# A two-layer scan kernel: the second layer's instructions in an order written out by hand, side work cut into small pieces, ten of sixteen states fed through TensorE

## The chip, the cores and the metric

The kernel runs on one core of a Trainium2 chip. A core has four engines that compute, each with its own instruction queue that is worked through strictly in order: TensorE (PE: matrix multiplies and transposes, with its weight loads shown apart as PEld), VectorE (DVE), ScalarE (ACT) and GpSimd (POOL). SyncE (SP) issues the DMAs. The metric is the device time of one execution in microseconds (us). Everything is float32.

## The reference, cut to what matters

There are two layers over an input of 2 batches x 2048 positions x 256 features. Layer 0 (a gated scan and a routed feed-forward) is not touched by the change. Layer 1 is a pair of selective scans, forward and backward in time, each over 512 channels with 16 states, followed by a norm, and two feed-forwards:

```python
xz = x @ Win;  xi, z = split(xz);  xi = silu(conv4(xi))       # depthwise, causal
dt = softplus((xi @ Wx)[:16] @ Wdt + bdt);  Bm, Cm = (xi @ Wx)[16:32], [32:48]
def step(h, u_t, dt_t, B_t, C_t):              # h: 512 channels x 16 states
    h = exp(dt_t * A) * h + (dt_t * u_t) * B_t
    return h, einsum('ds,s->d', h, C_t)
y = (scan(step) + u * D) * silu(z) @ Wout      # then layernorm, for both directions
out = layernorm(ff(yf + yb) + yf + yb) + x + gelu_ff(x)
```

## The kernel before

Layer 1 (function `layer1`, L495) handles time in chunks of T = 512 positions. Its **16 steps** are, for each of 2 batches, 4 chunks forward and 4 chunks backward (L630 to L635). A step has K = 64 **iterations**, one per pair of a state n (16) and a block e of 128 channels (4). An iteration is one 128x512 recurrence on VectorE (`scan`, L825, the instruction at L836).

Around each recurrence:

- `decay` (L797) makes exp(dt * A) on ScalarE (L806).
- `source` (L808) makes the input term dt * u * B. There are **two kinds of iteration**. In kind D, GpSimd multiplies `dtu` by a broadcast row of B (L823); the decay lies in PSUM, and the recurrence writes over it. In kind P ("turned B"), ScalarE first scales the transposed `dtuT` by a column of B (`scaled`, L788, at L792, four pieces per state, each serving four channel blocks), and TensorE transposes the result back into PSUM (L816, four 128x128 transposes); the recurrence writes to SBUF.
- After the recurrence its last column is copied to `hn`, for the next chunk (kind P: GpSimd, L844; kind D: ScalarE, L847), and the result is multiplied by a broadcast row of C (kind P: GpSimd, L845; kind D: VectorE, L848).
- `collect` (L850), some iterations later, adds the product to the output by four accumulating transposes on TensorE (L870).

Iterations come in eight blocks m of 8 (two states x four channel blocks). `kinds` (L755) says which kind each state has: DD, then six times PD (alternating), then PP. PSUM has eight banks: four for the output accumulators (`yacc`), two for side work (`pp`), and **two (`ab`) for the iterations**: the bank of iteration g is filled again for g+2 only when the recurrence of g (in kind D, also its C product) is over.

**Side work** goes between the iterations: `finish_parts` (L1063) of the step before (transposes, the output projection, norms and, where that step was a backward one, two halves of both feed-forwards, `ff_parts`, L925), `prepare_parts` (L1034) of the step after (gate and input projections, convolution, Silu, projections to dt, B, C, Softplus), a `prologue` in steps 4 to 7, and `late_parts` (L1056). Each part carries a weight, and the loop at L1094 to L1144 emits parts so that the weights are spread over iterations 5 to 55; `late_parts` is emitted at iteration 56. Steps 5 to 8 and 13 to 15 thus hold the feed-forwards of a backward chunk; I call them **ff steps**, and the others **plain steps**.

What is emitted is not yet the order on the engines: the tile framework's **planner** reorders the instructions of each engine by emission order, readiness and an estimate of costs, and allots the buffers. Decays are emitted 4 iterations ahead (kind P) or 1 ahead (kind D), sources 1 ahead, `collect` 4 behind.

Of the kernel before, what the change touches and what calls it, by code (L numbers as in the profile page):

```python
# [18 lines left out]
P = 128  # L19
# [475 lines left out]
def layer1(tc, c, a, x1d, wupd, wdnd, bupd, out):  # L495
    nc = c.nc
    with ExitStack() as ctx:
# [78 lines left out]
        zero = wp.tile([P, P], F32, name="zero")  # L576
        nc.gpsimd.memset(zero, 0.0)
        ident4 = c.ident.unsqueeze(1).broadcast_to([P, 4, P])
# [68 lines left out]
        def gate(ck, zs, tb):  # L647

            ps = c.pp()
            for k in range(2):  # L650
                nc.tensor.matmul(
                    ps, ck.xnT[:, k, tb * P : (tb + 1) * P], ck.w["winz"][:, k, :],
                    start=(k == 0), stop=(k == 1),
                )
            nc.scalar.copy(zs[:, tb, :], ps)

        def conv(i, e):
# [5 lines left out]
            ps = c.pp()  # L663
            for k in range(2):
                nc.tensor.matmul(
                    ps, w["winx"][:, k, e * P : (e + 1) * P], ck.xnT[:, k, :],
                    start=(k == 0), stop=(k == 1),
                )
# [11 lines left out]
            for k in range(3):  # L680
                o = 3 - k if bw else k
                nc.vector.scalar_tensor_tensor(  # L682
                    ck.u[:, e] if k == 2 else ps, xi[:, o : o + T], pk[:, e, k : k + 1], ps,
                    ALU.mult, ALU.add,
                )
# [5 lines left out]

        def project(i):
            ck = steps[i]
            ps = c.pp()
            for e in range(4):
                nc.tensor.matmul(  # L696
                    ps, ck.w["wx"][:, e, :], ck.u[:, e, :], start=(e == 0), stop=(e == 3)
                )
            ck.par = ap.tile([P, T], F32, tag="par", name="par", bufs=1)
            nc.scalar.copy(ck.par, ps)  # L700
            ck.bcd = c.dram.tile([80, T], F32, tag="bcd", name="bcd", bufs=3)
            nc.sync.dma_start(ck.bcd[32:80, :], ck.par[32:80, :])
# [52 lines left out]
        kinds = ["DD"] + ["PD"] * 6 + ["PP"]  # L755
# [9 lines left out]
        lo, hi = 0, 8  # L765
        for n in range(NS):
            ks = [k for k in range(K) if plan[k][1] == n and plan[k][3] == "P"]
            if ks:
                for q in range(TB):
                    fills[lo + q * (hi - lo) // TB].append((n, q))  # L770
                lo, hi = ks[0], ks[-1] + 1
# [25 lines left out]
        def decay(g):  # L797
# [4 lines left out]
            if kind == "P":  # L802
                r["a"] = sp.tile([P, T], F32, tag="a", name="a", bufs=5)
            else:
                r["a"] = r["ps"] = c.ab()
# [19 lines left out]
        def scan(g):  # L825
# [15 lines left out]
            gt = r["g"] = sp.tile([P, T], F32, tag="g", name="g", bufs=6)  # L841
            hn = ck.hn[:, e, n : n + 1]
            if kind == "P":
                nc.gpsimd.tensor_copy(hn, h[:, last : last + 1])  # L844
                nc.gpsimd.tensor_mul(gt, h, ck.cb[n])  # L845
            else:
                nc.scalar.copy(hn, h[:, last : last + 1])  # L847
                nc.vector.tensor_mul(gt, h, ck.cb[n])  # L848

        def collect(g):  # L850
# [3 lines left out]
            if k == 0:  # L854
# [3 lines left out]
                for tb in range(TB):  # L858
                    nc.tensor.matmul(
                        ck.y[tb], zero, ident4, start=True, stop=False, skip_group_check=True  # L860
                    )
                    for e2 in range(4):
# [3 lines left out]
                            start=False, stop=False, is_transpose=True, skip_group_check=True,  # L866
# [29 lines left out]
        def project_out(i, h):  # L896
# [3 lines left out]
            xn = tp.tile([P, 2, D], F32, tag="xn", name="xn", bufs=2)  # L900
            nc.sync.dma_start(xn, rows2(xn1d[ck.b], r))
            if ck.bw:
                yf = tp.tile([P, 2, D], F32, tag="yf", name="yf", bufs=2)
                nc.sync.dma_start(yf, rows2(yfd[ck.b][ck.k], h))
            ps = c.pp()
            for n in range(2):
                for e in range(4):
                    q = 2 * h + n
                    nc.tensor.matmul(  # L909
                        ps[:, n * D : (n + 1) * D], ck.ygT[:, e, q * P : (q + 1) * P],  # L910
                        ck.w["wout"][:, e, :], start=(e == 0), stop=(e == 3),
                    )
            nc.vector.tensor_add(xn, xn, ps.rearrange("p (n d) -> p n d", d=D))
            mv, rs = c.stats(tp, xn, 2)
            c.normalize(xn, xn, mv, rs, 2)
            if not ck.bw:
                nc.sync.dma_start(rows2(yfd[ck.b][ck.k], h), xn)
                return
            nc.vector.tensor_add(yf, yf, xn)
            nc.vector.tensor_mul(yf, yf, bcast(FW["fwnw"]))  # L920
            nc.vector.tensor_add(yf, yf, bcast(FW["fwnb2"]))
            ck.yf = ck.__dict__.setdefault("yfs", {})
            ck.yfs[h] = yf

        def ff_parts(i, h):  # L925
# [6 lines left out]
            def up(q):  # L932
                if q == 0:
                    S["g"] = tp.tile([P, 8, 256], F32, tag="big", name="gff")
                ps = c.pp()
                for j in range(2):
                    hd = 2 * q + j
                    for kk in range(2):
                        nc.tensor.matmul(
                            ps[:, j * 256 : (j + 1) * 256],  # L940
                            FW["wup"][:, kk, hd * P : (hd + 1) * P],
                            ck.xnT[:, kk, t0 : t0 + 256],
                            start=(kk == 0), stop=(kk == 1),
                        )
                for j in range(2):
                    hd = 2 * q + j
                    nc.scalar.activation(
                        S["g"][:, hd], ps[:, j * 256 : (j + 1) * 256], AF.Identity,
                        bias=FW["bup"][:, hd : hd + 1],
                    )  # L950

# [3 lines left out]
            def down():  # L955
                x1t = S["x1t"] = tp.tile([P, 2, D], F32, tag="x1t", name="x1t", bufs=2)
                nc.sync.dma_start(x1t, rows2(x1d[b], 2 * k + h))
                nc.gpsimd.tensor_add(x1t, x1t, bcast(FW["obias"]))
                ps = c.pp()
                for j in range(2):  # L960
                    for hd in range(8):
                        nc.tensor.matmul(  # L962
                            ps[:, j * D : (j + 1) * D], S["g"][:, hd, j * P : (j + 1) * P],
                            FW["wdn"][:, hd, :], start=(hd == 0), stop=(hd == 7),
                        )
                nc.vector.tensor_add(x1t, x1t, ps.rearrange("p (n d) -> p n d", d=D))
# [15 lines left out]
            def ff1(q):  # L982
                if q == 0:
                    S["h1"] = tp.tile([P, 4, 256], F32, tag="h1", name="h1")
                ps = c.pp()
                for j in range(2):
                    hd = 2 * q + j
                    for kk in range(2):
                        nc.tensor.matmul(
                            ps[:, j * 256 : (j + 1) * 256],  # L990
                            FW["w1"][:, kk, hd * P : (hd + 1) * P],
                            S["yT"][:, kk, :],
# [250 lines left out]
```

## Time and profile before

| what | us |
|---|---|
| median of 3 runs (lowest, highest) | 4129.29 (4126.32, 4132.78) |
| the profiled execution | 4139.88 |
| its span | 4138.2 |
| layer 0, until the first recurrence of layer 1 | 1647.0 |
| plain steps 1, 2, 3, 9, 10, 11 | 133.1 to 134.6 each |
| plain steps 0, 4 and 12 | 127.9, 136.0 and 129.0 |
| ff steps 5, 6, 7 (with a `prologue` each) | 181.0, 180.9, 180.9 |
| ff steps 8, 13, 14 | 170.4, 176.3, 177.3 |
| ff step 15, and the tail behind it | 139.1, 91.5 |

A step's time is the distance from its first recurrence to that of the next step, in the timeline of VectorE. The profile has a page (busy time by engine, then costliest groups) and views: windows (busy time of each engine in a stretch), groups by line, waits (who waited for whom), the chain of waits, and the timeline. Busy time is a union: an instruction's start overlaps the end of the one before it.

### The profile page before, as it was taken

What the parts mean: (1) busy time and instruction counts of PE and PEld (TensorE: products, weight loads), DVE (VectorE), ACT (ScalarE), POOL (GpSimd) and SP (SyncE); (2) the same over time, 40 slices, a digit from 0 to 9 for tenths busy, and PEclk for the clock granted to TensorE, in tenths of its full rate; (3) what the DMA queues carried; (4) which work ended last, traced back from release to release, by engine and by line L of the source; (5) the groups of instructions that cost most, each with busy time, mean ns of one, the idle gap of its engine ahead of it and who ended that gap; (6) DMA issues with size and microseconds to landing.
All of it is one profiled execution on the core that took longest, in us unless ns stands there. A gap on an engine that the chain in (4) does not pass through costs nothing.

```text
span 4138.2 us, 41758 instructions
## 1 busy us (share of the span) xinstructions
PE 2927.6 (71%) x13136; PEld 2056.6 (50%) x13136; DVE 3327.6 (80%) x4436; ACT 2353.4 (57%) x4721; POOL 2038.9 (49%) x2197
## 2 busy tenths in 40 slices
PE   6445364657677666777777778787877778888887
PEld 3323242434444433455555656575655555656565
DVE  7899999887988975888888767777788888767782
ACT  3433434354655654766766665655666766665662
POOL 5465555200000002677776656655577776656661
PEclk8657565657676676888889989898988888889898
DMA  4322142312122124312212121212121212111110
GB/s 135 119 96 67 59 125 102 100 44 76 32 66 67 34 59 128 101 60 66 61 60 75 59 73 46 78 56 69 52 67 60 63 65 70 54 52 52 47 46 13
DMA packets 170995, 285.07 MB, mean 69 GB/s; under 512 B 18571, under 2 KB 90443, under 8 KB 165644
## 3 DMA queue, kind: packets, MB, share of 16 engines
q1 hardware_dynamic: 170166, 280.30, 22.7%
q8 instruction: 104, 1.70, 0.2%
q0 software_dynamic: 608, 2.10, 0.1%
q14 instruction: 117, 0.96, 0.1%
HBM read 240.66 MB, written 24.91 MB: 64 GB/s over the span
## 4 chain that ended last, share of the span: by engine, by line
DVE 21%; PE 16%; POOL 9%; ACT 8%; issue 6%; DMA 0%; DVEq 0%; SPq 0%; POOLq 0%; ACTq 0%
DVE h L836 6%; DVE ab L836 6%; POOL g L845 3%; DVE g L848 3%; PE pp L962 3%; PE yacc L870 2%; POOL b L823 2%; PE ab L816 2%; ACT ab L806 2%; PE pp L696 2%; DVE pp L682 2%; PE pp L909 1%; POOL dtu L733 1%; ACT zu L690 1%; PE pp L1007 1%
## 5 line engine op out<-in xcount | busy, mean ns | idle before, releaser
L823 POOL TENSOR_TENSOR b<-dtu,bb 128x512 f32<-128x512 f32 x512 | 651.8, 1278 | 280.1 <-DVE ab L836 262.6
L427 PE MATMUL yacc<-da,ident 128*128 128x256 f32 x1024 | 449.9, 585 | 475.5 <-DVE da L424 410.2
L870 PE MATMUL yacc<-ident,g 128*128 128x128 f32 x4096 | 676.4, 302 | 144.2 <-POOL g L845 104.4
L870 PEld LDWEIGHTS yacc<-ident,g 128*128 128x128 f32 x4096 | 534.7, 156 | 264.4 <-POOL g L845 144.9
L845 POOL TENSOR_TENSOR g<-h,cb 128x512 f32<-128x512 f32 x512 | 651.8, 1273 | 0.4 <-POOL hc L844 0.2
L836 DVE TENSOR_TENSOR_SCAN h<-a,hc,ab 128x512 f32<-128x512 f32 x384 | 483.4, 1268 | 164.4 <-PE ab L816 155.1
L427 PEld LDWEIGHTS yacc<-da,ident 128*128 128x128 f32 x1024 | 268.5, 286 | 638.7 <-ACT hc L421 168.9
L816 PE MATMUL ab<-ident,bT 128*128 128x128 f32 x2048 | 373.1, 308 | 261.3 <-DVE h L836 168.5
L836 DVE TENSOR_TENSOR_SCAN ab<-ab,hc,b 128x512 f32<-128x512 f32 x384 | 485.5, 1277 | 70.7 <-ACT ab L806 68.0
L806 ACT ACTIVATE ab<-dt,A 128x512 f32<-128x512 f32 x512 | 351.5, 690 | 222.5 <-DVE h L836 113.0
L816 PEld LDWEIGHTS ab<-ident,bT 128*128 128x128 f32 x2048 | 264.9, 156 | 415.5 <-DVE h L836 243.2
L806 ACT ACTIVATE a<-dt,A 128x512 f32<-128x512 f32 x512 | 365.9, 717 | 160.5 <-DVE h L836 160.3
L417 DVE TENSOR_TENSOR_SCAN h<-da,h,bt 128x256 f32<-128x256 f32 x512 | 437.3, 891 | 8.9 <-ACT h L415 7.4
L64 POOL TENSOR_SCALAR rs<-mv 128x2 f32<-128x2 f32 (+1 forms) x72 | 16.6, 231 | 827.0 <-DVE mv L75 823.8
L401 ACT ACTIVATE da<-dt,A 128x256 f32<-128x256 f32 x512 | 235.1, 500 | 271.7 <-PE yacc L427 271.1
L848 DVE TENSOR_TENSOR g<-ab,cb 128x512 f32<-128x512 f32 x512 | 341.3, 678 | 55.3 <-ACT hc L847 54.9
L792 ACT ACTIVATE bT<-dtuT,BT 128x512 f32<-128x512 f32 x512 | 359.9, 717 | 10.5 <-PE ab L816 10.4
L405 DVE SCALAR_TENSOR_TENSOR bt<-dt,small,bt 128x256 f32<-128x256 f32 x512 | 333.3, 658 | 11.0 <-ACT bt L402 10.1
L844 POOL COPY hc<-h 128x1 f32<-128x1 f32 x512 | 103.1, 201 | 450.0 <-DVE h L836 407.6
L107 POOL TENSOR_TENSOR bft<-bfy,bfw 128x512 f32<-128x512 f32 (+1 forms) x100 | 158.6, 1604 | 321.9 <-DMA bfw<-in_upc_dram 165.9
L402 ACT ACTIVATE bt<-da,nc,c 128x256 f32<-128x256 f32 x512 | 280.6, 589 | 0.0
L847 ACT COPY hc<-ab 128x1 f32<-128x1 f32 x512 | 80.1, 157 | 253.4 <-DVE ab L836 251.1
(201 smaller groups left out, 5634.5 us busy)
## 6 DMA issues: line engine op xcount, KB each, us to landing
cb<-bcd SPq DMA_DIRECT2D x256, 256.0 KB
cb<-cd SPq DMA_DIRECT2D x128, 256.0 KB
bb<-bcd SPq DMA_DIRECT2D x128, 256.0 KB
bfw<-in_upc_dram SPq DMA_DIRECT2D x20, 1024.0 KB
bfw<-in_dnc_dram SPq DMA_DIRECT2D x20, 1024.0 KB
relay<-inter SPq DMA_DIRECT2D x128, 128.0 KB
f1c<-in_f_dram SPq DMA_DIRECT2D x8, 1024.0 KB
f2bd<-in_f_dram SPq DMA_DIRECT2D x16, 512.0 KB
```

Of the source, the lines that this page charges most:

```text
L402: nc.scalar.activation(bt[:, j], da[:, j], AF.Identity, scale=c1[:, e, s], bias=nc1[:, e, s])
L405: nc.vector.scalar_tensor_tensor(bt[:, j], dt[:, e], small[:, e, s], bt[:, j], ALU.mult, ALU.add)
L417: nc.vector.tensor_tensor_scan(h[:, j, 1 : LC + 1], da[:, j], bt[:, j], h[:, j, 0:1], ALU.mult, ALU.add,)
L427: nc.tensor.matmul(ys[e][:, 0:LC], c.ident, da[:, j], start=(n == 0), stop=(n == NS - 1))
L792: nc.scalar.activation(t, ck.dtuT[:, q, :], AF.Copy, scale=ck.BT[:, q, n : n + 1])
L806: nc.scalar.activation(r["a"], ck.dt[:, e], AF.Exp, scale=ck.w["A"][:, e, n : n + 1])
L816: nc.tensor.transpose(r["b"][:, q * P : (q + 1) * P], ck.bT[n, q][:, e * P : (e + 1) * P], c.ident,)
L823: nc.gpsimd.tensor_mul(r["b"], ck.dtu[:, e], ck.bb[n])
L836: nc.vector.tensor_tensor_scan(h[:, step], r["a"][:, step], r["b"][:, step], 0.0 if ck.first else steps[i - 1].hn[:, e, n : n + 1], ALU.mu ...
L845: nc.gpsimd.tensor_mul(gt, h, ck.cb[n])
L848: nc.vector.tensor_mul(gt, h, ck.cb[n])
L870: nc.tensor.matmul(ck.y[tb][:, e * P : (e + 1) * P], gt[:, tb * P : (tb + 1) * P], c.ident, start=False, stop=(k == K - 1), is_transpose=T ...
```

## The change

It has six parts:

1. The loop over the iterations runs under `tc.manual_schedule` for the four engines: each of them now takes its instructions in the order in which the code emits them. The DMAs on SP stay with the planner. The loop is rewritten: decays of kind P 5 iterations ahead (buffers for `a` from 5 to 6), `collect` 3 behind (buffers for `g` from 6 to 5).
2. Side work is cut into pieces of mostly one or two matmuls. A new function `spread` places them: everything ahead of `silus` over iterations 4 to 31, `silus` at 32, the projections over 32 to 47, `softplus` at 48, `late_parts` one by one over 56 to 63. `prologue` now comes ahead of `prepare_parts`.
3. `kinds` becomes DD PD PD PD PP PD PP PP: ten states of kind P rather than eight; `fills` is timed anew.
4. The copy of the last state in kind D goes from ScalarE to VectorE.
5. The matmul by `zero` that opened each output accumulator goes; the first transpose starts it.
6. Two 128x512 additions of each ff half go from VectorE to GpSimd.

```diff
-        kinds = ["DD"] + ["PD"] * 6 + ["PP"]
+        kinds = ["DD", "PD", "PD", "PD", "PP", "PD", "PP", "PP"]
...
-                r["a"] = sp.tile([P, T], F32, tag="a", name="a", bufs=5)
+                r["a"] = sp.tile([P, T], F32, tag="a", name="a", bufs=6)
...
-                nc.scalar.copy(hn, h[:, last : last + 1])
+                nc.vector.tensor_copy(hn, h[:, last : last + 1])
...
-                    nc.tensor.matmul(
-                        ck.y[tb], zero, ident4, start=True, stop=False, skip_group_check=True
-                    )
...
-                            start=False, stop=False, is_transpose=True, skip_group_check=True,
+                            start=(e2 == 0), stop=False, is_transpose=True,
+                            skip_group_check=True,
...
-            nc.vector.tensor_add(yf, yf, bcast(FW["fwnb2"]))
+                nc.gpsimd.tensor_add(yf, yf, bcast(FW["fwnb2"]))
...
-                nc.vector.tensor_add(y, y, S["x1t"])
+                nc.gpsimd.tensor_add(y, y, S["x1t"])
...
             return (
-                [(7, lambda q=q: up(q)) for q in range(4)]
-                + [(6, gelu), (7, down), (2, turn)]
-                + [(3.5, lambda q=q: ff1(q)) for q in range(2)]
-                + [(5, ff2)]
+                [(1, lambda hd=hd: up(hd)) for hd in range(8)]
+                + [(3, gelu)]
+                + [(1, lambda j=j, h2=h2: down(j, h2)) for j, h2 in pairs]
+                + [(0.3, down_add), (0.9, turn)]
+                + [(1, lambda hd=hd: ff1(hd)) for hd in range(4)]
+                + [(1, lambda j=j, h2=h2: ff2(j, h2)) for j, h2 in pairs if h2 < 4]
+                + [(0.7, norm), (1.5, store)]
             )
...
+            r += conv_parts(i)
+            r.append((("at", 32), lambda: silus(i)))
+            r += [(0.9, lambda e=e: project_mm(i, e)) for e in range(4)]
+            r.append((0, lambda: project(i)))
+            r += [(1, lambda e=e: delta(i, e)) for e in range(4)]
+            r.append((("at", 48), lambda: softplus(i)))
+            r.append((0.9, lambda: rowsB(i)))
...
+        AHEAD = {"P": 5, "D": 1}
+        BEHIND = 3
+        LATE = K - 8
...
+        with tc.manual_schedule(engines={nc.tensor.engine, nc.scalar.engine, nc.vector.engine, nc.gpsimd.engine}):
+            for g in range(-AHEAD["P"], N + BEHIND):
+                if 0 <= g < N:
+                    i, k = divmod(g, K)
+                    if k == 0:
+                        todo = spread(filler(i), BEHIND + 1, LATE - 4) + spread(late(i), LATE, K)
+                        todo.sort(key=lambda x: x[0])
+                    if k % 8 == 0 and k + 8 < K:
+                        load_bc(i, k // 8 + 1)
+                for kind, by in AHEAD.items():
+                    if 0 <= g + by < N and plan[(g + by) % K][3] == kind:
+                        decay(g + by)
+                if 0 <= g < N:
+                    for n, q in fills[k]:
+                        scaled(i, n, q)
+                if 0 <= g + 1 < N:
+                    source(g + 1)
+                if 0 <= g < N:
+                    scan(g)
+                if 0 <= g - BEHIND < N:
+                    collect(g - BEHIND)
+                if 0 <= g < N:
+                    while todo and todo[0][0] <= k:
+                        todo.pop(0)[1]()
```

In each step, iterations 4 to 31 so hold these pieces: in a plain step, per iteration 1 to 3 (in all 4 `turned`, 8 output projections, 8 gate and 8 input projections, 12 convolution taps, two norms); in an ff step, in addition 2 x (8 `up`, Gelu, 8 `down`, `turn`, 4 `ff1`, 4 `ff2`, a norm) and, in steps 5 to 7, the `prologue`. In step 15 nothing is prepared, and the pieces are spread over iterations 4 to 51.

## Prediction

> **What bounds the kernel now.** First the page's busy times; then the windows view, one stretch per step, because layer 1 mixes two sorts of step.
>
> ```profile
> span 4138.2 us, 41758 instructions
> ...
> PE 2927.6 (71%) x13136; PEld 2056.6 (50%) x13136; DVE 3327.6 (80%) x4436; ACT 2353.4 (57%) x4721; POOL 2038.9 (49%) x2197
> ```
>
> ```profile
> core 0: us, PE busy (x) PEld busy (x) DVE busy (x) ACT busy (x) POOL busy (x), PEclk, DMA share, GB/s
> 1913.02:2046.11 133.09, 101.80 (x524) 71.59 (x524) 113.53 (x127) 90.17 (x161) 95.13 (x117) 0.86 0.22 67
> 2496.24:2677.16 180.92, 147.01 (x732) 110.65 (x732) 129.34 (x165) 110.96 (x195) 105.19 (x129) 0.90 0.22 64
> ```
>
> No engine is full. A plain step (first row) has VectorE at 113.5 of 133.1 us, an ff step (second) PE at 147.0 of 180.9. The lost time is handing over. The waits view of the ff step shows what the recurrence waits for:
>
> ```profile
> DVE h L836 <- PE ab L816: 13.0, 6, 6.8
> DVE ab L836 <- ACT ab L806: 8.6, 5, 4.7
> DVE g L848 <- ACT hc L847: 6.1, 14, 1.9
> DVE x1t L966 <- PE pp L962: 5.8, 2, 2.9
> ```
>
> Few waits, but long ones: the recurrence stands up to 6.8 us behind PE, which is inside one piece of side work (the 32 matmuls of L962 stand as 7.2 us in one go in the chain of waits). Next, blocks of eight iterations (first recurrence to first recurrence), from the timeline. Plain step 2: 16.9, 18.4, 16.5, 19.0, 17.4, 13.0, 19.4, 12.4. Ff step 6: 16.9, 24.6, 22.4, 17.0, 28.4, 25.2, 24.9, 21.5. So a PD block without VectorE side work takes 13.0. Three of these blocks, by windows (plain DD, plain last, ff fifth):
>
> ```profile
> 1909.49:1926.40 16.91, 13.57 (x73) 9.67 (x74) 16.05 (x20) 13.59 (x28) 10.67 (x10) 0.90 0.20 62
> 2030.10:2042.58 12.48, 11.06 (x77) 9.64 (x75) 10.20 (x10) 7.26 (x12) 10.80 (x16) 0.87 0.23 64
> 2573.60:2602.00 28.40, 26.35 (x135) 20.41 (x134) 17.25 (x26) 18.96 (x32) 14.36 (x17) 1.00 0.12 28
> ```
>
> DD is VectorE's (16.05 of 16.91); the ff block is PE's at 93%.
>
> **Prices.** From starts of neighbours in the timeline:
>
> ```profile
> 2033.62 5.96 DVE L836 TENSOR_TENSOR_SCAN h<-a,hc,ab 128x512 f32<-128x512 f32 x5 [1.57 <-PE ab L816]
> 2044.93 1.26 DVE L848 TENSOR_TENSOR g<-ab,cb 128x512 f32<-128x512 f32 x2
> 1988.54 1.28 ACT L690 ACT_TABLE_LOAD   x1
> 1989.83 3.62 ACT L690 ACTIVATE zu<-zu 128x4096 f32<-128x4096 f32 x1
> ```
>
> VectorE: a recurrence every 1.19 us, a C product 0.63. GpSimd: copy and product of a P iteration 1.35 (copies L844 start at 2039.02, 2040.38, 2041.73), B product of a D iteration 1.25 (two in 2.51). PE at full clock: transpose 0.109, 512-column pass 0.429, 256-column pass 0.216 (a matmul is two passes). ScalarE: decay or `scaled` piece 0.72, table load 1.28, Silu 3.62, Softplus and Gelu 1.91.
>
> **Part 4, the copies.** VectorE's copy of one column isn't in the trace. Nearest row: aggregate L75, 164 ns, less the overlap of some 60 ns: 0.10 us. From above: a normalize (L82) takes 411 ns by its median but 757 on average in layer 1 (to 1484) beside GpSimd, so a copy held like that costs 0.35 more. From below: it replaces a wait, 2.1 us per plain and 6.1 per ff step. I take 0.10, so a D iteration is 1.19+0.10+0.63 = 1.92; the upper end, 24 x 0.35 = 8.4 us on 16 steps, 134 us, goes into the range. The Trainium skill (VectorE: DVE Perf Modes, "Why PSUM operands drop a tier") lets the two-port mode run only with operands in SBUF, and this copy reads PSUM: by it the hold and the 134 us are nothing; no row here shows a copy of that kind.
>
> **Part 3, states.** Eight D iterations per step become P. VectorE loses 8 x 0.63, GpSimd swaps 8 x 1.25 for 8 x 1.35, PE gains 32 transposes (3.5), ScalarE 8 pieces (5.8) less 32 copies of 0.16 (5.1). What counts is where: a PP block is 8 x 1.35 = 10.8 on GpSimd against 9.5 on VectorE, so GpSimd sets it.
>
> **Parts 1 and 2, a plain step, block by block.** In order, each engine looks one to three iterations ahead. The DMAs stay with the planner on SP; the waits view of the ff step names none, so I cost them at nothing (a load of `x1t` or `xn` issued late would stand at the head of GpSimd's or VectorE's queue; that is in rival 2).
> - DD: 16.9 plus 8 copies: 17.6.
> - Iterations 8 to 31: 12 x 1.19 + 12 x 1.92 = 37.3; 12 taps x 0.67 = 8.0; two norms of 2.35 (add 0.63, stats 0.70, aggregates 0.20, normalizes 0.82); 2.4 of waits for GpSimd's rstd, as now. 52.4. PE has under 40 here.
> - Iterations 32 to 39: Silu on ScalarE from the last tap: 1.28+3.62. The first `project_mm` waits for it at the head of PE's queue, ahead of the source of 34, so 34 starts 4.9+0.9+0.7 = 6.5 after 32 and six follow at 1.25: 14.0. Now 17.4.
> - 40 to 47: 13.0.
> - 48 to 55: Softplus and two table loads (4.5), a decay and a piece behind it: the source of 52 comes 6.7 after 48, then 4 x 1.35: 12.1. Now 19.4.
> - 56 to 63: GpSimd does 10.8, and in the same queue `delta_u` 4 x 1.25 and `skip_term` 4 x 0.65, ahead of the next step's first B product: 18.4. Now 12.4, since the planner put `delta_u` earlier (2018 to 2023, while VectorE stood).
>
> Sum 127.5 against 133.1: **-5.6**. Seven steps (1 to 4, 9 to 11): -39; step 12, now 129.0: -2. Step 0, mostly start-up: 0.
>
> **An ff step.** The second half is the same, 57.5. The first holds nearly all side work:
> - 0 to 3: 4 x 1.92 and four gated products x 0.63: 10.2.
> - 4 to 7: VectorE 4 x 1.92 + 2 x (2.35 + 1.24): 14.9.
> - 8 to 23: PE, 47 pieces of four 256-column passes (0.86) = 40.6, and 104 transposes = 11.4: 52; at the 93% of the ff block above, 56. Twice the first `down` stands at the head of PE's queue behind table load and Gelu, 3 each: 62.
> - 24, 25: recurrences 3.1, norm and store 3.0, `prologue` norms 3.4, three rstd waits of 1.2: 13.
> - 26 to 31: PE 16 x 0.86 + 36 transposes: 17.7, VectorE 17.3.
>
> Sum 117.8+57.5 = 175.3 against 180.9: -5.6, three times: -17. Without the prologue (5.8) 169.5: -1, -7, -8 on steps 8, 13, 14. Step 15, spread over 48 iterations: 17.6, four PD blocks of 12.4, three PP of 10.8, norms 14.4, rstd 4.8, Gelu 6: 125 against 139: -14. Part 6 saves 4 x 0.67 on VectorE, already left out above; in the tail GpSimd's 1.27 stands for 0.67, +1. Part 5 takes 4.8 us off PE (L859, 8 x 0.6) where VectorE is the bound: nothing, and if PE were late there, up to that per step.
>
> -39-2-17-1-7-8-14+1 = -87: span 4051. The profiled execution is 1.7 us over its span and 0.26% over the median of the runs shown: (4051+1.7) x 4129.29/4139.88 = **4042**.
>
> **A rule against part 3.** The second half feeds PE almost only transposes. The trace has such a stretch:
>
> ```profile
> 2034.00:2046.00 12.00, 8.48 (x64) 6.58 (x62) 11.38 (x11) 8.88 (x17) 11.04 (x16) 1.00 0.13 39
> 1986.00:1999.00 13.00, 9.73 (x33) 6.48 (x32) 9.25 (x11) 9.11 (x9) 5.43 (x7) 0.50 0.08 21
> ```
>
> The first holds 64 transposes and nothing else on PE, at clock 1.00; half clock (0.50, second row; 0.213 per transpose) comes around the Silu, when PE stands. The Trainium skill (TensorE: Matmul & The Clock Gate, "Part 4: PE-mode transpose") says that transposes don't bring the full clock. By it a P iteration's eight would take 1.7 us instead of 0.9, 0.35 over GpSimd's 1.35: 24 such iterations in 15 steps, +126, or 4168. I go by the row.
>
> **Rivals.**
> 1. *The queues run ahead of one another*, so that a step is nearer to each engine's own sum than to a sum of stretches. For: the ff block at 93%. Against: two `ab` banks and in-order queues. Plain: 17.6+52.4 and GpSimd's 50.4 from iteration 32 on (28 x 1.35 + 4 x 1.25 + 7.6): 120.4. Ff: PE's iterations 4 to 31 hold 72 pieces of 0.86 and 196 transposes, 83; 10.2 + 83/0.93 + 6 + 50.4 = 156. -97, then -75, -15, -20, -21, -18: -246, **3883**.
> 2. *Slower: the crammed first half of an ff step.* Side work that now lies over 51 iterations gets 28, and within one iteration pieces depend on each other: matmul, ScalarE copy 0.59, Identity 0.76, taps 2.0 on VectorE; norm, rstd, normalize. If nothing overlaps across iterations: 22.5 for 4 to 7 (two of 7.0, VectorE waiting for rstd), 66 for 8 to 23, 15 for 24 and 25, 28 for 26 to 31 (four convolution blocks of 5.3 behind two gate iterations of 3.5): 142 with the first four, a step of 199. Then +19 three times, +22, +15, +14, and -5 for step 15 (a third of the 14 left), plain steps even: +103, **4232**. It decides once iterations 0 to 31 take over 123.4 (180.9-57.5); my forecast has 117.8, so it is near.
> 3. *Even*: the planner's order was already as good, and gain and loss cancel: **4129**.
>
> **Chances.** Forecast 0.40 (4000 to 4090), rival 1 0.29 (3840 to 3960), rival 2 0.25 (4180 to 4290), rival 3 0.06 (within 0.2%, about what a measurement tells from no change). Faster 0.69, same 0.06, slower 0.25. The range 3865 to 4225 leaves out some 0.07 of rival 1 and half of rival 2.
>
> **What would show it.** Plain steps at 125 to 130, last block near 18 with GpSimd full, `hc` copies near 0.1 us on VectorE, fifth block 14. Ff steps: iterations 0 to 31 near 118 with PE about 90% busy in 8 to 23. Wrong if the copies take 0.3 or more, if PE's clock stays at 0.50 in the PP blocks, or if VectorE's waits move to the taps and normalizes of iterations 4 to 31.

## The result, and the profile after

The changed kernel takes **4477.57 us** (4 runs, 4476.9 to 4478.23) against 4131.03 of the kernel before beside it: ratio 1.0838, 95% interval 1.0819 to 1.0857. It is 347 us slower. The forecast was 4042, the range ended at 4225, and rival 2, the slower one, said 4232: direction and size are both missed.

The page of the kernel after, its span, busy times and the shares of the chain of waits:

```profile
span 4476.5 us, 42608 instructions
...
PE 3010.2 (67%) x13520; PEld 2151.8 (48%) x13520; DVE 3322.2 (74%) x4660; ACT 2378.3 (53%) x4336; POOL 2075.4 (46%) x2356
...
PE 24%; DVE 16%; ACT 11%; POOL 10%; issue 3%; DMA 0%; SPq 0%; POOLq 0%; DVEq 0%; ACTq 0%
```

VectorE works 3322 us, as before (3328); the other engines gain 25 to 83. No engine has 347 us more to do. In the chain PE has gone from 16% to 24% and VectorE from 21% to 16%. The windows of the kernel after, the same two steps as before (plain step 2, ff step 6):

```profile
1936.04:2084.49 148.45, 106.97 (x548) 79.30 (x548) 114.88 (x142) 91.22 (x136) 95.67 (x125) 0.79 0.17 53
...
2606.83:2823.45 216.62, 156.97 (x756) 118.50 (x756) 130.31 (x176) 113.17 (x170) 109.34 (x141) 0.83 0.17 51
```

The columns are as in the prediction: stretch, sum, then PE, PEld, VectorE, ScalarE, GpSimd, granted clock. A plain step takes 148.5 instead of 133.1, an ff step 216.6 instead of 180.9, with VectorE at 114.9 and 130.3 (before 113.5 and 129.3). So the loss is idle time of VectorE. From the gaps of its timeline: 19.6 us before, 33.6 after in step 2; 51.6 before, 86.3 after in step 6. In both steps the growth is mostly gaps ahead of recurrences (14.8 to 28.9; 24.5 to 51.0). The blocks of eight iterations:

| block | 0-7 | 8-15 | 16-23 | 24-31 | 32-39 | 40-47 | 48-55 | 56-63 |
|---|---|---|---|---|---|---|---|---|
| plain, before | 16.9 | 18.4 | 16.5 | 19.0 | 17.4 | 13.0 | 19.4 | 12.4 |
| plain, forecast | 17.6 | 52.4 | (sum of three) | | 14.0 | 13.0 | 12.1 | 18.4 |
| plain, after | 20.9 | 22.0 | 18.1 | 19.4 | 16.2 | 19.0 | 13.0 | 19.9 |
| ff, before | 16.9 | 24.6 | 22.4 | 17.0 | 28.4 | 25.2 | 24.9 | 21.5 |
| ff, after | 33.4 | 34.9 | 31.8 | 48.5 | 16.7 | 18.6 | 12.9 | 19.9 |

Three plain blocks of the kernel after, by windows (40 to 47, 48 to 55, 56 to 63):

```profile
2032.69:2051.68 18.99, 15.53 (x56) 9.53 (x56) 12.83 (x18) 12.25 (x20) 12.12 (x15) 0.64 0.26 80
2051.68:2064.63 12.95, 10.19 (x67) 8.83 (x68) 9.80 (x9) 12.89 (x18) 9.70 (x15) 0.86 0.14 48
2064.63:2084.49 19.86, 14.08 (x88) 11.32 (x85) 9.91 (x8) 7.96 (x14) 19.72 (x26) 0.83 0.12 29
```

The last two are full of one engine, ScalarE (12.89 of 12.95) and GpSimd (19.72 of 19.86): these came nearly as forecast. The first is full of none: PE, the busiest, has 15.53 of 18.99, at a granted clock of 0.64. The same block before, from which the forecast took its 13.0:

```profile
1997.70:2010.70 13.00, 12.30 (x60) 7.23 (x59) 12.02 (x13) 10.55 (x20) 10.54 (x12) 0.94 0.27 90
```

What VectorE waits for, in the waits of the whole execution, before and after:

```profile
DVE h L836 <- PE ab L816: 202.2, 130, 9.1
DVE ab L836 <- ACT ab L806: 89.5, 118, 4.9
...
DVE ab L836 <- POOL b L823: 22.2, 4, 21.4
```

```profile
DVE ab L864 <- ACT ab L834: 192.0, 70, 5.9
DVE h L864 <- PE ab L844: 163.0, 88, 5.4
DVE ab L864 <- POOL b L851: 152.1, 52, 24.0
DVE x1t L1006 <- PE pp L999: 88.9, 16, 16.4
...
DVE pp L698 <- ACT pp L689: 49.0, 15, 6.1
```

L864 is the recurrence (L836 before), L834 the decay (L806), L844 the transposes of kind P (L816), L851 the source of kind D (L823). Two lines have grown most. The wait for a kind-D source is 129.9 us longer; 114.5 of its 152.1 stand ahead of the first recurrences of the 16 steps, behind GpSimd's last block, which the forecast had counted (18.4 instead of 12.4). The wait for a decay, 102.5 us longer, needs an explanation, since ScalarE is idle 47% of the time. The timeline of the plain block 40 to 47 shows one such wait:

```profile
2040.84 2.07 PE L747 MATMUL pp<-par,wdt 16*128 16x512 f32 x2
...
2042.94 0.69 ACT L750 ACTIVATE dt<-pp,pk 128x512 f32<-128x512 f32 x1 [3.27 <-PE pp L747]
...
2043.53 0.71 ACT L834 ACTIVATE a<-dt,A 128x512 f32<-128x512 f32 x1
...
2044.14 0.68 ACT L834 ACTIVATE ab<-dt,A 128x512 f32<-128x512 f32 x1
...
2044.93 1.29 DVE L864 TENSOR_TENSOR_SCAN ab<-ab,hc,b 128x512 f32<-128x512 f32 x1 [2.88 <-ACT ab L834]
```

The matmul of a `delta` piece (L747) runs on PE at 2040.84. ScalarE's Identity on its result (L750) is next in ScalarE's written order and holds that queue for 3.27 us; behind it stand the decays of the next iterations, and behind the second of them the recurrence, for 2.88. The delay went from PE to ScalarE to VectorE: PE and GpSimd worked meanwhile, and ScalarE and VectorE stood. In the ff step the queues of PE and VectorE do it too:

```profile
2689.76 3.51 PE L999 MATMUL pp<-wdn,gff 128*128 128x256 f32 x8 [2.91 <-ACT gff L990]
...
2697.17 0.60 PE L844 MATMUL ab<-ident,bT 128*128 128x128 f32 x4
...
2699.98 0.69 DVE L1006 TENSOR_TENSOR x1t<-x1t,pp 128x512 f32<-128x512 f32 x1 [5.47 <-PE pp L999]
2700.58 1.27 DVE L864 TENSOR_TENSOR_SCAN h<-a,hc,ab 128x512 f32<-128x512 f32 x1
```

`down`'s matmuls first wait 2.91 for Gelu, then `down_add` waits 5.47 for them at the head of VectorE's queue, and the recurrence behind it starts with no wait of its own. Its source (the line between) had ended at 2697.77, so some 2.2 us of the 5.47 are lost to the place in VectorE's queue; until then the source itself stood in PE's, behind 16 of `down`'s matmuls.

### The profile page after: what moved, and what is told of

Same layout as the page of the kernel before. It is cut to its first block, busy times and chain, and to the rows that moved or that the text cites. A ratio compares the mean times of both kernels' runs of the same rounds, so it can differ in the third digit from the quotient of the medians.

```text
span 4476.5 us, 42608 instructions
## 1 busy us (share of the span) xinstructions
PE 3010.2 (67%) x13520; PEld 2151.8 (48%) x13520; DVE 3322.2 (74%) x4660; ACT 2378.3 (53%) x4336; POOL 2075.4 (46%) x2356
## 4 chain that ended last, share of the span: by engine, by line
PE 24%; DVE 16%; ACT 11%; POOL 10%; issue 3%; DMA 0%; SPq 0%; POOLq 0%; DVEq 0%; ACTq 0%
POOL g L873 5%; DVE ab L864 5%; PE yacc L896 4%; PE ab L844 4%; PE pp L999 3%; DVE h L864 3%; PE pp L978 2%; DVE g L876 2%; ACT bT L820 2%; PE pp L649 2%; ACT a L834 2%; PE pp L720 2%; POOL dtu L761 2%; DVE pp L698 1%; PE pp L747 1%
## 5 line engine op out<-in xcount | busy, mean ns | idle before, releaser
L873 POOL TENSOR_TENSOR g<-h,cb 128x512 f32<-128x512 f32 x640 | 813.8, 1272 | 0.4 <-POOL hc L872 0.2
L896 PE MATMUL yacc<-ident,g 128*128 128x128 f32 x4096 | 718.5, 307 | 108.7 <-POOL g L873 108.3
L864 DVE TENSOR_TENSOR_SCAN h<-a,hc,ab 128x512 f32<-128x512 f32 x480 | 598.3, 1269 | 193.4 <-PE ab L844 122.3
L844 PE MATMUL ab<-ident,bT 128*128 128x128 f32 x2560 | 468.9, 309 | 295.3 <-DVE h L864 199.3
L864 DVE TENSOR_TENSOR_SCAN ab<-ab,hc,b 128x512 f32<-128x512 f32 x288 | 369.4, 1283 | 281.0 <-ACT ab L834 152.1
L844 PEld LDWEIGHTS ab<-ident,bT 128*128 128x128 f32 x2560 | 340.6, 158 | 472.5 <-DVE h L864 233.7
L851 POOL TENSOR_TENSOR b<-dtu,bb 128x512 f32<-128x512 f32 x384 | 485.4, 1271 | 64.2 <-DVE ab L864 64.2
L834 ACT ACTIVATE a<-dt,A 128x512 f32<-128x512 f32 x640 | 453.5, 713 | 29.4 <-DVE h L864 28.8
L834 ACT ACTIVATE ab<-dt,A 128x512 f32<-128x512 f32 x384 | 264.8, 690 | 369.5 <-DVE g L876 368.1
L820 ACT ACTIVATE bT<-dtuT,BT 128x512 f32<-128x512 f32 x640 | 450.8, 709 | 19.0 <-PE ab L844 19.0
L405 DVE SCALAR_TENSOR_TENSOR bt<-dt,small,bt 128x256 f32<-128x256 f32 x512 | 332.9, 657 | 12.4 <-ACT bt L402 11.6
L876 DVE TENSOR_TENSOR g<-ab,cb 128x512 f32<-128x512 f32 x384 | 262.2, 683 | 5.0 <-PE yacc L896 4.7
L864 DVE TENSOR_TENSOR_SCAN h<-a,ab 128x512 f32<-128x512 f32 x160 | 189.7, 1209 | 69.7 <-PE ab L844 40.8
```

The costliest lines, as they stand in the source:

```text
L405: nc.vector.scalar_tensor_tensor(bt[:, j], dt[:, e], small[:, e, s], bt[:, j], ALU.mult, ALU.add)
L820: nc.scalar.activation(t, ck.dtuT[:, q, :], AF.Copy, scale=ck.BT[:, q, n : n + 1])
L834: nc.scalar.activation(r["a"], ck.dt[:, e], AF.Exp, scale=ck.w["A"][:, e, n : n + 1])
L844: nc.tensor.transpose(r["b"][:, q * P : (q + 1) * P], ck.bT[n, q][:, e * P : (e + 1) * P], c.ident,)
L851: nc.gpsimd.tensor_mul(r["b"], ck.dtu[:, e], ck.bb[n])
L864: nc.vector.tensor_tensor_scan(h[:, step], r["a"][:, step], r["b"][:, step], 0.0 if ck.first else steps[i - 1].hn[:, e, n : n + 1], ALU.mu ...
```

## The experiments

Two sorts of theory were to be told apart. **Hand-over**: in the written order a piece and the instruction that takes over its result stand in one iteration, so that the taking-over engine stands at the head of its queue, with decays and recurrences behind it. **Content**: what the other parts put there (ten states, copies, fixed places, cramming) is slower in any order. "Over before" is against the kernel before in the same job; it ran at 4131 to 4139 from job to job, so differences between times of two jobs are good to some 8 us.

### Which part loses: the order taken off, and parts by themselves

**e1**, the whole change with the planner's order:

```diff
-        with tc.manual_schedule(engines={nc.tensor.engine, nc.scalar.engine, nc.vector.engine, nc.gpsimd.engine}):
+        if True:
```

> All of the change but the hand-written order: the planner orders all engines again. Theory A (the order itself is the loss: within one iteration the queues stand behind each other): most of the 347 us comes back, 4050 to 4180, with plain steps at 125 to 135 us and ff steps at 170 to 190. Theory B (the content is the loss: side work crammed into iterations 4 to 31, GpSimd's late parts, ten states of kind P): the planner can't mend it, over 4350, and the last block of a step stays near 20 us.

Measured: 4347.92, ratio 1.0512 (1.0494 to 1.0531), 214 over before. Plain step 2: 144.9, with 20.8, 26.1 and 13.5 in the last three blocks; ff step 6: 197.2. Both theories missed: too little comes back for A, and for B the last block should have stayed near 20. The written order costs some 130 here, and the rest of the change 214 by itself.

**e5** and **e6**, in the kernel before: the states of part 3 with their `fills`, and the copy of part 4.

```diff
-        kinds = ["DD"] + ["PD"] * 6 + ["PP"]
+        kinds = ["DD", "PD", "PD", "PD", "PP", "PD", "PP", "PP"]
```

> The kernel before with part 3 alone: ten states of kind P with the new order of kinds and the new fills, planner and coarse side work as before. Theory B1 (the mix of kinds is the loss that the planner run kept): 4250 to 4350. Theory B2 (the mix is harmless, the placement of the side work is the loss): 4090 to 4160; by the sums of the prediction VectorE loses 5 us a step.

```diff
-                nc.scalar.copy(hn, h[:, last : last + 1])
+                nc.vector.tensor_copy(hn, h[:, last : last + 1])
```

> The kernel before with part 4 alone: the 32 copies per step of a kind-D recurrence's last column on VectorE. The trace after shows a copy at 160 ns, and recurrence, copy and product of a D iteration in 2.0 instead of 1.82 us: 32 x 0.19 = 6 us a step, 96 us, less the waits for ScalarE's copy that go (55 us in all): 4150 to 4190. If the freed ScalarE counts: under 4120.

Measured: e5 4191.49, 1.0149 (1.013 to 1.0168), 60 over before; the four last blocks of step 2 are 11.6, 19.0, 19.1 and 18.2 instead of 17.4, 13.0, 19.4 and 12.4. e6 4141.08, 1.0022 (1.0013 to 1.0032), 10 over before. Each lies between the two values expected for it. The states take 5 us per step off VectorE (108.3 busy in step 2) and all of that, and more, comes back as waiting.

**e8** and **e11**, under the planner with Silu and Softplus as ordinary weights in an even placement over iterations 4 to 51; e11 in addition with the states of before and the copies on ScalarE, so that the small pieces, the distances 5 and 3, and parts 5 and 6 are left.

```diff
-            r.append((("at", 32), lambda: silus(i)))
+            r.append((5, lambda: silus(i)))
...
-            r.append((("at", 48), lambda: softplus(i)))
+            r.append((3, lambda: softplus(i)))
```

> The same placement under the planner (both part 1's order and the fixed places undone). If placement is what the planner run still lost: 4100 to 4180, near the kernel before. If the mix of kinds or the copies are: above 4250.

> The even placement under the planner, with eight states of kind P and the copies on ScalarE as before: what is left of the change is the small pieces with their new weights, decays 5 ahead, collect 3 behind, no zero matmul, four additions per ff step on GpSimd. If states (60 us alone) and copies (10 us alone) add up to the 120 us of the even planner run only with a loss of the pieces: 4160 to 4200. If the two make it together: 4110 to 4140.

Measured: e8 4250.92, 1.0291 (1.0276 to 1.0306), 120 over before; e11 4173.30, 1.0077 (1.0059 to 1.0095), 34 over before. So under the planner: small pieces and what goes with them 34; states and copies bring it to 120, 86 more (60 and 10 by themselves); the fixed places, with the cramming of iterations 4 to 31, to 214.

**e12**, part 5 alone in the kernel before:

```diff
-                    nc.tensor.matmul(
-                        ck.y[tb], zero, ident4, start=True, stop=False, skip_group_check=True
-                    )
...
-                            start=False, stop=False, is_transpose=True, skip_group_check=True,
+                            start=(e2 == 0), stop=False, is_transpose=True, skip_group_check=True,
```

> The kernel before with part 5 alone: no matmul by zero, the first transpose starts the accumulator. 128 passes of 0.6 to 0.75 us go from PE at the head of each step, where VectorE is the bound: 4115 to 4135, faster by up to 0.3%; the planner may deal out another order, which moves a step by a few us either way.

Measured: 4126.29 against 4139.09 in the same job, 0.9973 (0.9962 to 0.9984): 13 us faster. It is the only version here that beats the kernel before.

### Cramming, and the place of the pieces in the written order

**e7** is the whole change in its written order, with e8's even placement; **e2** writes the pieces of an iteration ahead of its source, recurrence and `collect` instead of behind them.

> The change, but Silu and Softplus lose their fixed places at iterations 32 and 48: with weights 5 and 3 they and all side work are spread evenly over 4 to 51, hand-written order kept. If cramming into 4 to 31 is the loss: ff steps fall from 216 to 185 to 200 us, the total to 4250 to 4380; plain steps even, or some us worse where Silu meets kind-D decays. If the amount of side work times a fixed cost of handing over is the loss, wherever it lies: ff steps stay at 210 to 220, total within 1% of 4478.

> The hand-written order kept; in each iteration the side work is emitted ahead of source, scan and collect instead of behind them. Theory A in its ScalarE form (a side piece waits on PE behind source and collect, its copy on ScalarE waits for it, and the next kind-D decay stands behind that copy): the chain is cut, plain PD blocks fall from 18 to 22 us to 14 to 17, total 4250 to 4380. If instead the sums of work by stretch set the time (theory B): within 1% of 4478. Against it: VectorE's own side work now stands ahead of the recurrence it used to follow, which could cost 50 us.

Measured: e7 4466.04, 1.0813 (1.0797 to 1.083): no more than 12 us from the crammed one. e2 4579.65, 1.1078 (1.1061 to 1.1096): worse by 102. Under the planner the even placement is worth 94 (214 less 120), under the written order next to nothing: with it the order costs 215 (4251 to 4466). So cramming, on which rival 2 rested, isn't what the written order loses by.

e2's total missed its theory, but its trace shows both halves of it. The wait for decays falls from 192.0 to 30.8, and block 40 to 47 of step 2 takes 13.4 at a granted clock of 1.00, against 19.0 at 0.64, with the same pieces: the chain through ScalarE is cut there. In its place the pieces now stand ahead of the recurrence's own source and on VectorE ahead of the recurrence: the wait behind PE's transposes rises from 163.0 to 299.2 and that of the first tap behind `conv`'s Identity from 49.0 to 127.3. In step 6 iterations 0 to 31 take 166.2 instead of 148.5.

### Which queue

The same kernel with the order of some engines left to the planner: **e3** without ScalarE, **e4** without PE, **e9** without VectorE, **e10** without PE and ScalarE, **e15** with VectorE alone in the written order. The diff of e9 stands for all:

```diff
-        with tc.manual_schedule(engines={nc.tensor.engine, nc.scalar.engine, nc.vector.engine, nc.gpsimd.engine}):
+        with tc.manual_schedule(engines={nc.tensor.engine, nc.scalar.engine, nc.gpsimd.engine}):
```

> ScalarE alone goes back to the planner; PE, VectorE and GpSimd keep the hand-written order. If ScalarE's queue is where the loss is made (decays behind copies of side work), 4150 to 4300. If PE's queue is (a side matmul waiting for Gelu, Silu or a copy stands ahead of sources), 4400 to 4478.

> PE alone goes back to the planner; the other three keep the hand-written order. If PE's queue is where the loss is made, 4150 to 4300. If ScalarE's queue is, 4400 to 4478: ScalarE waits in the same order whatever PE does first.

> The change with VectorE alone given back to the planner; PE, ScalarE and GpSimd in the hand-written order. Freeing ScalarE gave nothing and freeing PE cost 60 us. If the loss of the order lies in VectorE's own queue (a ready recurrence behind a tap, an addition or a normalize that waits): 4350 to 4420, at best the planner run's 4348. If the engines hold each other and no single queue is at fault: 4440 to 4520.

> PE and ScalarE together given back to the planner, VectorE and GpSimd in the hand-written order. If the chain PE to ScalarE and back is the loss and one alone can't be mended while the other stays: 4340 to 4400. If VectorE's order is the loss: 4440 or more.

> The whole change, but only VectorE takes its instructions in the written order; the other three are left to the planner. All four free gave 4348, all but VectorE written 4400, all written 4478. If VectorE's written order costs by itself what freeing it gave back: 4348 + 78 = 4426. If it costs only together with the written order of the engines that feed it: 4350 to 4375.

| written order on | us | ratio (interval) |
|---|---|---|
| all four (the change) | 4477.57 | 1.0838 (1.0819 to 1.0857) |
| all but ScalarE (e3) | 4475.34 | 1.0826 (1.0809 to 1.0842) |
| all but PE (e4) | 4537.70 | 1.0975 (1.0957 to 1.0993) |
| all but VectorE (e9) | 4399.61 | 1.0626 (1.0608 to 1.0644) |
| VectorE and GpSimd (e10) | 4438.49 | 1.0723 (1.0707 to 1.0738) |
| VectorE alone (e15) | 4412.24 | 1.0677 (1.0655 to 1.0698) |
| none (e1) | 4347.92 | 1.0512 (1.0494 to 1.0531) |

No single queue holds the loss. Of 130, freeing VectorE gives back 78, and VectorE's order alone costs 64; both readings put about half on VectorE's queue. e4 lies outside both ranges stated for it, e10 and e15 fall between theirs. Freeing ScalarE alone gives nothing, which spoke against ScalarE's queue as the one cause; freeing PE alone makes it worse by 60, I suppose because its order then no longer fits the others'. This is what one expects of a delay that runs through several queues, but it doesn't show it.

### The hand-overs taken out

**e13** keeps the written order on all four engines and writes no piece in the same iteration as the piece that it waits for. ScalarE's copies out of PSUM go into a list that is emitted in the next iteration, behind its recurrence; pieces marked `wait` are left for the next iteration if something has been emitted in this one. At a step's last iteration all that is left is written out at once. In a plain step Silu and Softplus stay where they were (iterations 32 and 49 in the trace); in step 6 Silu slips to 46. **e14** is the same with e7's even placement.

```diff
+        def defer(f):
+            pend.append(f) if live[0] else f()
...
-            nc.scalar.copy(ck.ygT[:, e, :], ps)
+            defer(lambda: nc.scalar.copy(ck.ygT[:, e, :], ps))
...
-                (0.5, norm), (1, store)
+                (0.5, wait(norm)), (1, wait(store))
...
-                    while todo and todo[0][0] <= k:
+                    for f in pend[:]:
+                        f()
+                    pend.clear()
+                    fresh = False
+                    while todo and todo[0][0] <= k and len(pend) < 2:
+                        if fresh and hasattr(todo[0][1], "wait"):
+                            break
                         todo.pop(0)[1]()
+                        fresh = True
```

> The whole change in its written order on all four engines, but no piece of side work is written in the same iteration as the piece that it waits for: an instruction that takes over a result from another engine (ScalarE's copies out of PSUM, the adds and normalizes of the norms, the first tap, the first matmul behind a Silu, Gelu or Relu) is written one iteration after its producer, behind that iteration's recurrence. Theory A, the loss of the written order is the hand-over inside one iteration, which holds the queue of the engine that takes it over and the recurrence behind it: plain step from 148.5 to 140 or less, ff step from 216.6 to 195 or less, about 4478 - 8 x 9 - 8 x 20 = 4250. Rival B, it is the order of recurrence, copy and C product themselves: no change, 4440 to 4490. Between them, by the part that hand-overs have in it.

> The same with the side work spread evenly over iterations 4 to 51, Silu and Softplus among it (under the written order without the shift this was 4466, under the planner 4251). Theory A: 4250 or a little less, since the shift has room here. Rival B: 4430 to 4480.

Measured: e13 **4287.84**, 1.0378 (1.0357 to 1.0399); e14 4280.28, 1.0354 (1.0332 to 1.0376). That is 190 and 186 us less than the same kernels without the shift (4477.57 and 4466.04). Plain step 2 went from 148.5 to 136.9, ff step 6 from 216.6 to 199.6, nearly as the hand-over theory had it (140, 195; 4250). The waits of e13, whose lines are 9 to 18 lower down:

```profile
DVE ab L876 <- POOL b L863: 163.5, 55, 26.8
DVE h L876 <- PE ab L856: 161.1, 107, 6.1
DVE x1t L1024 <- PE pp L1017: 118.1, 14, 16.4
...
DVE ab L876 <- ACT ab L846: 66.2, 14, 5.2
...
DVE pp L707 <- ACT pp L698: 7.1, 3, 6.2
```

Waits of the recurrence behind a decay fell from 192.0 in 70 to 66.2 in 14, those of the first tap behind `conv`'s Identity from 49.0 to 7.1. The first three lines are as long as before the shift, or longer. The wait for a kind-D source is GpSimd's last block, which e18 below takes up; the two behind PE I read as PE's matmuls themselves, but no run shows that.

**e17** asks whether what VectorE's freedom gave back was the same loss: e13 with VectorE left to the planner.

```diff
-        with tc.manual_schedule(engines={nc.tensor.engine, nc.scalar.engine, nc.vector.engine, nc.gpsimd.engine}):
+        with tc.manual_schedule(engines={nc.tensor.engine, nc.scalar.engine, nc.gpsimd.engine}):
```

> The kernel of e13 (hand-overs written one iteration later), with VectorE's own order left to the planner. Without the shift, freeing VectorE gave back 78 us. If that was the same loss that the shift removes, little of it is left: 4265 to 4300, within 25 us of e13's 4288. If VectorE's written order holds a loss of its own, another 50 or more comes back: 4240 or less.

Measured: 4315.89, 1.0444 (1.0429 to 1.046), 28 more than e13. That is outside both ranges, but the question is answered: where freeing VectorE gave 78 back without the shift, it now costs 28, so nothing of the 78 is left once the hand-overs are shifted.

### The states under the written order, and the last block

**e16** is the whole change in its written order with the states of before; **e18** is e13 with `delta_u` and `skip_term` on VectorE.

```diff
-        kinds = ["DD", "PD", "PD", "PD", "PP", "PD", "PP", "PP"]
+        kinds = ["DD"] + ["PD"] * 6 + ["PP"]
```

> The whole change in its written order, but with the eight states of kind P of before (DD, six PD, PP). The two further states cost 60 us by themselves under the planner. If that adds up with the order's loss: about 4418, plain steps near 144.5. If the states' cost lies in what the planner makes of the last blocks, which the written order avoids: 4470 or more.

```diff
-            nc.gpsimd.tensor_mul(ck.dtu[:, e], ck.dt[:, e], ck.u[:, e])
+            nc.vector.tensor_mul(ck.dtu[:, e], ck.dt[:, e], ck.u[:, e])
...
-            nc.gpsimd.tensor_scalar(
+            nc.vector.tensor_scalar(
```

> The kernel of e13, with the four products of delta_u and the four of skip_term on VectorE instead of GpSimd. In e13 the last block of a step still takes 19.8 to 20.3, and I put that down to GpSimd's queue (8 x 1.35 and 4 x 1.25 + 4 x 0.65), while VectorE needs 9.5 there. If so, the last block falls to VectorE's 9.5 + 4 x 0.63 + 4 x 0.45, about 14, and the kernel by 15 x 5.5 = 80, to about 4205. If the block is bound by the recurrence's exchange of two banks with PE, or by the transposes of dtu behind the last fills, it stays near 20 and the kernel within 4270 to 4300.

Measured: e16 4474.44, 1.0829 (1.0808 to 1.085): as the change itself. Under the written order the two further states neither cost nor bring anything, though VectorE then works 120.4 us in step 2 instead of 114.9: step 2 is 1.9 longer, its waiting 3.5 shorter. e18 **4214.66**, 1.0191 (1.0169 to 1.0213), 73 less than e13, where 80 were expected. The last block of step 2, e13 and then e18:

```profile
2030.93:2050.96 20.03, 14.38 (x84) 11.68 (x84) 9.79 (x10) 7.61 (x13) 19.78 (x26) 0.80 0.13 29
```

```profile
2028.26:2043.95 15.69, 12.31 (x87) 9.98 (x84) 13.94 (x18) 7.65 (x14) 15.30 (x19) 0.89 0.13 37
```

GpSimd filled the block (19.78 of 20.03), and with seven instructions fewer the block is 4.3 us shorter, GpSimd again at 15.30. The whole execution's wait for a kind-D source falls from 163.5 to 72.9. Plain steps 1 to 3 and 9 to 11 now take 131.7 to 133.9, no more than before; what is left of the loss, 82 us, lies in the ff steps (195.9 in step 6 against 180.9) and in steps 0, 4, 12 and 15.

## Why the prediction was wrong

**The step that failed** is the sum in "Parts 1 and 2": block by block, each block at the time of its busiest engine or of a head-of-queue wait that I had listed (Silu, Softplus, Gelu, rstd). It took for granted that all other hand-overs are hidden since "each engine looks one to three iterations ahead". Emitted ahead are decays and sources; the pieces of side work are not. Each piece that passes from PE to ScalarE or on to VectorE within one iteration is a head-of-queue wait too, and I left those out, though rival 2 named them for the ff step. Writing them one iteration apart gives back 190 us (e13) and 186 (e14). That is 190 of the 436 us between the forecast of 4042 and the 4478 measured. The other 246 the shift doesn't reach: with it a plain step is still 9.4 over the forecast (136.9 against 127.5) and ff step 6 24.3 over (199.6 against 175.3), and what holds the ff steps stays open.

- *Block 40 to 47 of the plain step: 13.0, measured 19.0.* The price was that of "a PD block without VectorE side work" in the trace of before. This block has four `delta` pieces behind PE, and in the written order they hold up ScalarE's decays: ScalarE stands 93.1 us ahead of the 64 Identities (L750) of the whole execution. With the shift (e13) it takes 15.9, with the pieces ahead of the source (e2) 13.4.
- *DD: 17.6 (16.9 and 8 x 0.10 are 17.7), measured 20.9; iterations 8 to 31: 52.4, measured 59.5; Silu block: 14.0, measured 16.2.* With the shift: 18.9, 52.9 and 15.5. Iterations 8 to 31 then take what was forecast; that is the forecast's sum without hand-overs.
- *First half of an ff step: 117.8, measured 148.5.* Rival 2 had 142 from the mechanism that e13 and e17 confirm: pieces that depend on each other within one iteration, and no overlap across iterations. Iterations 0 to 7 were 25.1 in the forecast, 32.7 in rival 2 and 33.4 on the chip; iterations 24 to 31 were 30.7 in the forecast, 43 in rival 2 and 48.5 on the chip. In iterations 8 to 23 (66.7; forecast 62, rival 2 66) PE is busy 79%, not the 93% that I carried over from a block in the planner's order. Where rival 2 was wrong is the premise "plain steps even", and the word crammed: spreading the pieces out gave 12 of 347 us (e7).
- *Second half: 57.5, measured 68.1*; 5.6 of these 10.6 us lie in the block 40 to 47.
- *Right:* the last two blocks (12.1 and 18.4 forecast, 13.0 and 19.9 measured, ScalarE and GpSimd full), with e18 confirming the reason for the last one. In block 48 to 55 ScalarE is full throughout, where the forecast had GpSimd set the second half, and the 6.7 us stated for its first half are 0.8 more than the items listed for it (4.5 and 2 x 0.72). The clock in the two PP blocks was 0.86 and 0.83, not 0.50, and GpSimd filled the last of them, so the price of a P iteration by the row held and not the one by the rule weighed there. DMAs, put at nothing, took next to nothing: the largest wait of VectorE for one in layer 1 is 6.3 us in total, for `x1t`.
- *Part 4:* 0.10 us per copy; measured 0.158 each, and a D iteration from recurrence to recurrence takes 2.00 (2044.93 to 2046.93) instead of 1.82, so +0.18. All 384 copies lie between 157 and 160 ns, 243 of them beside a busy GpSimd: the upper end of 0.35 more is out. This agrees with the Trainium skill's rule on operands in PSUM (VectorE: DVE Perf Modes, "Why PSUM operands drop a tier"); no run has such a copy from SBUF to compare. Alone part 4 costs 10 us (e6).
- *Part 3* turns two blocks from PD to PP; these were forecast at 14.0 and 12.1 instead of 17.4 and 19.4, the fixed places included. Under the planner it costs 60 (e5), under the written order nothing (e16). VectorE was not full in these two blocks before (13.55 of 17.40 and 12.38 of 19.40), and less work on it became more waiting.
- *Part 5:* nothing expected, and up to 4.8 per step if PE were late; 13 us in all (e12), about 0.8 per step.
- *Rival 3's premise*, "the planner's order was already as good", was the better half of the truth: on the same pieces the planner is 130 to 215 us better than the written order. But the change loses 214 before any order is written, and I had only gains for that part. Nor is a written order worse as such: with the shift it is 60 us better than the planner's at the fixed places (e13 4288, e1 4348) and 29 worse at the even ones (e14 4280, e8 4251).

How the 214 under the planner split between fixed places and cramming isn't settled: e8 removes both at once. Part 6 was never run by itself. Also open is what holds the ff steps of e18 at 195.9; their waits name `down`'s matmuls (14.9 in step 6, before 5.8) and PE's transposes (14.9, before 13.0), but no run took these away. That e13 spreads the ff pieces over more iterations as well as shifting them is a second difference there; e14 against e7, both already spread, gives the same 186, so I hold the shift to be the cause.

## What to carry to other kernels

- Under in-order queues, a written order must be pipelined piece by piece: write the instruction that takes over a result one iteration later than the one that makes it, behind that iteration's critical instruction. Here that alone was worth 190 of 347 us, with the same number of instructions on every engine.
- Sum a step not by its busiest engines alone; list each producer and consumer that stand next to each other in the written order, and ask what is queued behind the consumer. A block's price from a trace in a planner's order needn't hold in another: block 40 to 47, priced 13.0, took 19.0, 15.9 or 13.4 by the place of its pieces.
- Take a bundled change apart before forecasting gains: six parts here held one that brings 13 us, and taking work off the busiest engine brought nothing where it waits for another.

## What was unexpected of the hardware

- A one-column copy on VectorE behind the recurrence that writes the column starts only when the recurrence has ended (at 2046.25, for a recurrence from 2044.93 that takes 1.29; in 383 of 384 measured, 33 to 35 ns after the end), though the recurrence of another tile starts 1.19 to 1.2 us after its predecessor. The product behind the copy so starts 1.40 us after the recurrence, and the D iteration is 0.18 longer.
- The granted clock of one block differs much with the order: 0.64 in block 40 to 47 of the plain step, against 0.94 before, 0.73 in e13 and 1.00 in e2; 0.68 in DD, against 0.90 before. Two matmul records with 16 rows and 512 columns took 2.07 us in that block. Whether the lower clock adds to the loss or only follows from it no run separates.
